# The first blocks of a fused macaron layer: normalization on another engine, ternary weights in quarters, and matmuls ahead of the first work

## The chip, the cores and the metric

The kernel runs on one core of one Trainium2 chip. A core has five engines, each with its own queue of instructions that it works off in order: PE (TensorE, matrix multiplication; its weight loads are shown as PEld), DVE (VectorE), ACT (ScalarE), POOL (GpSimd) and SP (SyncE, which here issues transfers only). They wait for each other through semaphores. SBUF is the working memory, 128 partitions wide, and PSUM the memory into which PE writes.

The metric is the device time of one execution in microseconds (us). The median of three runs of the kernel before is 625.42 us (625.16 to 626.89).

## The reference

An input x of 16 sequences of 256 tokens with 256 features goes through three residual blocks: half a feed-forward network (FFN), causal attention with 16 heads and rotary positions, and the same half FFN again. In front of each block stands a layer normalization. The weights of the FFN are made ternary first: each entry becomes -1, 0 or 1, by a threshold of half the mean absolute value of the whole matrix.

```python
def _bit_quant(w):
    scale = jnp.maximum(jnp.mean(jnp.abs(w)), EPS)
    w_ternary = jnp.clip(jnp.round(w / scale), -1.0, 1.0)
    return w + jax.lax.stop_gradient(w_ternary - w)
...
h = jnp.einsum('bsd,fd->bsf', x, w1q) + b1
h = jax.nn.gelu(h, approximate=False)
return jnp.einsum('bsf,df->bsd', h, w2q) + b2
...
x = x + 0.5 * _L0_ffn_ref(_layernorm(x, axis=-1), w1, b1, w2, b2)
x = x + _L0_attn_ref(_layernorm(x, axis=-1), Wq, Wk, Wv, Wo)
x = x + 0.5 * _L0_ffn_ref(_layernorm(x, axis=-1), w1, b1, w2, b2)
```

A layer normalization subtracts from each token its mean over the 256 features and multiplies by rstd, one over the root of its variance plus 1e-5.

## The kernel before

The 4096 tokens stand in SBUF for the whole kernel, as eight blocks `xs[0]` to `xs[7]` of 512 tokens (four tiles of 128 tokens each). All engines are called through `InOrder`, so that each engine's instructions stand in the order in which the program text issues them: what a line waits for, everything behind it on the same engine waits for too.

**Loads.** SP issues the loads in the order: first half of block 0, half of w1, the bias b1, w2, the bias b2, blocks 1 to 7, and then the attention's weights. ACT's queue issues the other half of block 0 and of w1. Meanwhile POOL sets the constants: the identity for transposes, `averaging` (a 128x128 matrix of one value), masks, `power` (the exponent -0.5).

**The FFN.** `ffn(ln, after)` makes one pass: `ln` is 0 for the first FFN and 2 for the second. `begin` does what precedes the first step, and `step(u)` is called for u = 0 to 65. Step u = 8 i + f does `up(i, f)` for block i and slice f of the 1024 hidden features (128 of them), and `down(i, f)` of the step two before (LATE = 2). `up` is four matmuls of 128x512 into a PSUM tile `m` (two of them at a time), then ACT's Gelu twice (`h_high`, in the rounded format that PE takes fast, and `h_whole`), and then the difference `h_rest`, on POOL for slices 1, 3 and 5 and on DVE otherwise. `down` is eight matmuls of 128x256 (`w<-w2q,h_high` and `w<-w2q,h_rest`). After the last slice of a block DVE adds the result to x.

**What has to be there first.** For each block: `stats` (two DVE instructions a tile), `finish_stats` (two POOL instructions of 128x4, `var` and `rstd`), `prepare` (four normalized tiles `xn`, by `normalize` on DVE), and `turn_in` twice (four transposes on PE, a cast on ACT, a difference on DVE), which gives `xnT`, what `up` multiplies. For block 1 all statistics are taken at step 1, `prepare` stands at step 3, and the `turn_in`s at steps 5 and 6, between `up` and `down`. For block 2 the statistics stand at steps 4 to 7, and so on.

For the weights: `sizes(n)` sums the absolute values of w1 (n = 0) or w2 (n = 1) by partition, `threshold(n)` sums over the partitions by two small matmuls with `averaging` and makes `half[n]`, and `signs(n, part)` makes the ternary values of a part by two DVE instructions. Before, these are halves of the matrix:

```python
signs(0, lambda w: w[:, :, 0 : FF // 2])        # in begin
signs(0, lambda w: w[:, :, FF // 2 :])          # in begin
if ln == 0 and u in (0, 3):                     # in step
    part = slice(0, NFC // 2) if u == 0 else slice(NFC // 2, NFC)
    signs(1, lambda w: w[:, part, :])
```

`add_bias(i)` lets POOL add half of b2 to the block's x, before the FFN's result is added.

**Behind the first FFN** the attention is written out in slots, which begin while the first FFN's last steps run, and then the second FFN. None of that is touched.

Of the kernel before, what the change touches and what calls it, by code (L numbers as in the profile page):

```python
# [8 lines left out]
FP = mybir.dt.float32  # L9
FR = mybir.dt.float32r  # L10
AF = mybir.ActivationFunctionType
ALU = mybir.AluOpType
# [17 lines left out]
def kernel(  # L30
# [144 lines left out]
    def tokens(n):  # L175
        return xs[n // BT][:, n % BT, :]

    def stats(ln, n):
        st = small.tile([P, 6], FP, name="st")
        vector.bn_stats(st, tokens(n))  # L180
        vector.bn_aggr(mv[ln][:, n, :], st)

    def finish_stats(ln, first, n):

        var = small.tile([P, BT], FP, name="var")
        gpsimd.tensor_scalar(
            var[:, 0:n], mv[ln][:, first : first + n, 1], LN_EPS, 1.0, ALU.add, ALU.mult
        )
        gpsimd.tensor_tensor(
            rstd[ln][:, first : first + n], var[:, 0:n], power[:, 0:n], ALU.pow  # L190
        )

    def normalize(ln, n, to, engine=None):
        (engine or vector).tensor_scalar(
            to,
            tokens(n),
            mv[ln][:, n, 0:1],
            rstd[ln][:, n : n + 1],
            ALU.subtract,
            ALU.mult,  # L200
        )
# [6 lines left out]
    def sizes(n):  # L208
        for k in range(2):
            part = (flat1, flat2)[n][:, k * FF : (k + 1) * FF]  # L210
            total = totals[n][:, k : k + 1]
            if n == 0 and k == 0:
                vector.tensor_reduce(total, part, AX.X, ALU.add, apply_absolute_value=True)
            else:

                size = w2q[:, k * NFC // 2 : (k + 1) * NFC // 2, :]
                scalar.activation(
                    size.rearrange("p k d -> p (k d)"), part, AF.Abs, accum_out=total
                )

    def threshold(n):
        mean = ps_mm.tile([P, 1], FP, name="mm")
        for k in range(2):
            total = totals[n][:, k : k + 1]
            tensor.matmul(mean, averaging, total, start=(k == 0), stop=(k == 1))

        for k, factor in enumerate((0.5, -0.5)):
            vector.tensor_scalar(
                half[n][:, k : k + 1], mean, QUANT_EPS, factor, ALU.max, ALU.mult
            )  # L230

    def signs(n, of):

        w, to = of((w1, w2)[n]), of((w1q, w2q)[n])
        vector.tensor_scalar(to, w, half[n][:, 1:2], None, ALU.is_lt)
        vector.scalar_tensor_tensor(
            to, w, half[n][:, 0:1], to.bitcast(FP), ALU.is_gt, ALU.subtract
        )
# [34 lines left out]
    def ffn(ln, after):  # L273
        xn, xnT, hT, ys = {}, {}, {}, {}

        def measure(i):
            if ln == 0:
                for t in range(BT):
                    stats(0, i * BT + t)
                finish_stats(0, i * BT, BT)  # L280

        def prepare(i, engine=None):
            xn[i] = fp.tile([P, BT, D], FP, name="xn", bufs=1)
            for t in range(BT):
                normalize(ln, i * BT + t, xn[i][:, t, :], engine)
            xnT[i] = [fp.tile([P, KC, TB], FR, name=f"xnT_{n}") for n in range(2)]

        def add_bias(i):
            gpsimd.tensor_add(xs[i], xs[i], b2_sb.unsqueeze(1).to_broadcast([P, BT, D]))

        def turn_in(i, k):
            tp = ps_mm.tile([P, TB], FP, name="mm")
            for t in range(BT):
                tensor.transpose(
                    tp[:, t * P : (t + 1) * P], xn[i][:, t, k * P : (k + 1) * P], ident
                )
            high, rest = (xnT[i][n][:, k, :] for n in range(2))
            scalar.copy(high, tp)
            return lambda: vector.tensor_sub(rest, tp, high.bitcast(FP))

        def up(i, f):
            h = ps_m.tile([P, TB], FP, name="m")
            for n in range(2):
                for k in range(KC):
                    tensor.matmul(
                        h,
                        w1q[:, k, f * P : (f + 1) * P],
                        xnT[i][n][:, k, :],
                        start=(n == 0 and k == 0),
                        stop=(n == 1 and k == KC - 1),  # L310
                    )
            high = fp.tile([P, TB], FR, name="h_high", bufs=LATE + 3)
            rest = fp.tile([P, TB], FR, name="h_rest", bufs=LATE + 3)
            whole = fp.tile([P, TB], FP, name="h_whole", bufs=3)
            scalar.activation(high, h, AF.Gelu, bias=b1_sb[:, f : f + 1])
            scalar.activation(whole, h, AF.Gelu, bias=b1_sb[:, f : f + 1])

            engine = gpsimd if f in (1, 3, 5) and not (ln == 0 and i == NBLK - 1) else vector
            engine.tensor_sub(rest, whole, high.bitcast(FP))
            hT[i, f] = (high, rest)  # L320

        def down(i, f):
            if f == 0 and ln == 2 and i == NBLK - 1:

                ys[i] = [ps_mm.tile([P, 2, D], FP, name="mm") for t in range(0, BT, 2)]
            elif f == 0:
                y = ps_w.tile([P, BT, D], FP, name="w")
                ys[i] = [y[:, t : t + 2, :] for t in range(0, BT, 2)]
            parts = hT.pop((i, f))
            order = [(t, n) for t in range(BT) for n in range(2)]  # L330
            if ln == 2 and (i, f) == (NBLK - 1, NFC - 1):

                order = [(t, n) for n in range(2) for t in range(BT)]
            for t, n in order:

                tensor.matmul(
                    ys[i][t // 2][:, t % 2, :],
                    parts[n][:, t * P : (t + 1) * P],
                    w2q[:, f, :],
                    start=(f == 0 and n == 0 and t % 2 == 0),  # L340
                    stop=(f == NFC - 1 and n == 1 and t % 2 == 1),
                )
            if f == NFC - 1:
                for t in range(0, BT, 2):
                    xt = xs[i][:, t : t + 2, :]
                    vector.scalar_tensor_tensor(
                        xt, ys[i][t // 2], 0.5, xt, ALU.mult, ALU.add
                    )
                for t in range(0, BT, 2):
                    after(i, t)  # L350

        def begin():
            measure(0)
            if ln == 0:
                sizes(0)
            prepare(0)
            if ln == 0:
                threshold(0)
                signs(0, lambda w: w[:, :, 0 : FF // 2])
            for k in range(KC):  # L360
                turn_in(0, k)()
            if ln == 0:
                signs(0, lambda w: w[:, :, FF // 2 :])
                sizes(1)

        def step(u):
            i, f = divmod(u, NFC)
            if i < NBLK:
                up(i, f)
                if ln == 0 and u == 0:  # L370
                    threshold(1)
                if ln == 0 and u in (0, 3):
                    part = slice(0, NFC // 2) if u == 0 else slice(NFC // 2, NFC)
                    signs(1, lambda w: w[:, part, :])
                if ln == 0 and u == 4:
                    gpsimd.tensor_scalar(b2_sb, b2_sb, 0.5, 0.0, ALU.mult, ALU.add)
                if u == 1:
                    measure(1)
                if ln == 0 and f >= 4 and i + 2 < NBLK:
                    stats(0, (i + 2) * BT + f - 4)  # L380
                    if f == NFC - 1:
                        finish_stats(0, (i + 2) * BT, BT)
                if i + 1 < NBLK:
                    if f == 3:
                        prepare(i + 1)
                    if f in (5, 6):
                        turn_in(i + 1, f - 5)()
                if f == (1 if i == NBLK - 1 else 6):
                    add_bias(i)
            if u >= LATE:  # L390
                down(*divmod(u - LATE, NFC))
            if ln == 0 and u == 2 * NFC + 2:
                make_tables()
            if ln == 0 and u < (NBLK - 1) * NFC and later:
                later.pop(0)()

        return begin, step, prepare, turn_in
# [423 lines left out]
```

## Time and profile before

| What | us |
|---|---|
| median of three runs (lowest, highest) | 625.42 (625.16, 626.89) |
| the profiled execution | 622.22 |
| its span, from the first to the last instruction | 620.4 |
| PE busy | 599.5 |
| DVE busy | 461.2 |
| ACT busy | 416.3 |
| POOL busy | 300.9 |

A profile is one execution, recorded instruction by instruction. Its span is shorter than the time of that execution, as the time also holds what lies around the first and the last instruction. All start times below count from the span's start. Every compute instruction of the kernel is recorded under line 167, the helper `traced`, so instructions are told apart by their tiles: `xn<-x,mv,rstd` is the instruction that writes `xn` from x, mean and variance, and rstd. A row of the timeline gives start, time from the first start to the last end, engine, line, operation, tiles, shapes and the number of instructions merged in it; in brackets, the time that the engine was idle before, and what ended it. "issue" is time in which an engine waited for nothing that the profile shows.

### The profile page before, as it was taken

Reading aid. Unit: us, or ns where it says so; the run is one execution under the profiler, and the core shown is the slowest. Engines: PE = TensorE matmul, PEld = TensorE weight load, DVE = VectorE, ACT = ScalarE, POOL = GpSimd, SP = SyncE. Lnnn points to the kernel's source line nnn. Section 1 sums busy time; section 2 is a strip of 40 time slices with the busy share of each in tenths; the row PEclk is TensorE's granted clock in tenths of the full one; section 3 lists DMA queues with packets and bytes.
Section 4 is the critical chain, followed back from the end, with each engine's and each line's share of the span. In section 5 each row is a group of like instructions: output and inputs, shape, how many; then the busy total and the mean of one; then the engine's idle time right before and its main releaser. Section 6 shows DMA issues by size and latency. Waiting matters only on the chain.

```text
span 620.4 us, 14716 instructions
## 1 busy us (share of the span) xinstructions
PE 599.5 (97%) x5580; PEld 486.6 (78%) x5580; DVE 461.2 (74%) x1654; ACT 416.3 (67%) x716; POOL 300.9 (49%) x273
## 2 busy tenths in 40 slices
PE   4999999999999999999999999999998999999997
PEld 3798999887667777777777777777766798888886
DVE  6877777786788888888888888888886465555553
ACT  4666766664576677676777677767765676676674
POOL 3655555782464455545564456453430243334443
PEclk9999999999999999999999999999999999999999
DMA  8800000000001000100001000100100011011001
GB/s 285 180 22 1 2 1 18 17 1 18 20 35 38 19 21 36 38 27 29 19 36 38 20 20 36 37 20 21 36 4 2 1 35 35 34 35 35 27 21 55
DMA packets 25478, 21.30 MB, mean 34 GB/s; under 512 B 10944, under 2 KB 21056, under 8 KB 25408
## 3 DMA queue, kind: packets, MB, share of 16 engines
q1 hardware_dynamic: 24848, 19.44, 9.8%
q8 instruction: 44, 0.72, 0.5%
q10 hardware_dynamic: 560, 0.92, 0.4%
q14 instruction: 26, 0.21, 0.1%
HBM read 7.51 MB, written 4.19 MB: 19 GB/s over the span
## 4 chain that ended last, share of the span: by engine, by line
PE 89%; DVE 5%; ACT 3%; issue 1%; DMA 1%; POOL 1%; DVEq 0%; SPq 0%; POOLq 0%
PE mm L167 38%; PE w L167 29%; PE m L167 22%; DMA w<-in_w1T_dram 1%; DVE h_rest L167 1%; DVE xn L167 1%; ACT h_high L167 1%; ACT h_whole L167 1%; DVE w2q L167 1%; DVE st L167 1%; DVE w L167 0%; DVE x L167 0%; DVE masked L167 0%; DVE mv L167 0%; ACT pT L167 0%
## 5 line engine op out<-in xcount | busy, mean ns | idle before, releaser
L167 DVE CUSTOM_DVE_ANT_0 masked<-m,mask_q 128x128 f32<-128x128 f32 x480 | 142.7, 354 | 41.0 <-PE m L167 39.7
L167 PE MATMUL m<-xnT,w1q 128*128 128x512 f32 x512 | 145.1, 404 | 0.8 <-ACT xnT L167 0.7
L167 ACT ACTIVATE h_high<-m,b_sb 128x512 fp32r<-128x512 f32 x128 | 88.5, 691 | 78.2 <-PE m L167 78.1
L167 DVE TENSOR_TENSOR h_rest<-h_whole,h_high 128x512 fp32r<-128x512 f32 x83 | 75.0, 904 | 72.0 <-ACT h_whole L167 71.5
L167 ACT ACTIVATE pT<-w 128x768 f32<-128x768 f32 x128 | 104.1, 815 | 31.4 <-DVE w L167 24.9
L167 PE MATMUL w<-qT,kT 32*128 32x256 f32 (+1 forms) x1024 | 120.6, 348 | 1.9 <-ACT pT L167 1.8
L167 PE MATMUL w<-w2q,h_high 128*128 128x256 f32 x480 | 120.8, 285 | 0.7 <-DVE w2q L167 0.7
L167 PE MATMUL w<-w2q,h_rest 128*128 128x256 f32 x480 | 117.8, 279 | 0.4 <-POOL h_rest L167 0.3
L167 PEld LDWEIGHTS w<-qT,kT 32*128 32x128 f32 x1024 | 89.9, 184 | 33.0 <-issue 25.9
L167 PE MATMUL m<-kT,qT 32*128 32x128 f32 x960 | 114.9, 349 | 0.7 <-ACT kT L167 0.7
L167 POOL TENSOR_TENSOR h_rest<-h_whole,h_high 128x512 fp32r<-128x512 f32 x45 | 60.1, 1335 | 108.5 <-ACT h_whole L167 108.4
L167 PEld LDWEIGHTS m<-xnT,w1q 128*128 128x128 f32 x512 | 88.3, 190 | 16.7 <-DVE xnT L167 2.9
L167 PEld LDWEIGHTS w<-w2q,h_rest 128*128 128x128 f32 x480 | 90.4, 188 | 5.1 <-POOL h_rest L167 0.7
L167 PEld LDWEIGHTS w<-w2q,h_high 128*128 128x128 f32 x480 | 90.3, 188 | 5.2 <-DVE w2q L167 1.2
L167 DVE TENSOR_TENSOR w<-w,mask_k 128x512 f32<-128x512 f32 x128 | 88.8, 695 | 7.1 <-PE w L167 7.0
L167 ACT ACTIVATE h_whole<-m,b_sb 128x512 f32<-128x512 f32 x128 | 87.3, 682 | 0.0
L167 PEld LDWEIGHTS m<-kT,qT 32*128 32x128 f32 x960 | 65.9, 185 | 2.9 <-ACT kT L167 1.6
L167 POOL TENSOR_TENSOR w<-w,cosT 128x512 f32<-128x512 f32 x32 | 41.3, 1292 | 51.8 <-ACT w L167 31.9
L167 PE MATMUL mm<-xnT_a,wqk 128*128 128x256 f32 x256 | 62.2, 386 | 0.0
L167 POOL TENSOR_SCALAR var<-mv 128x4 f32<-128x4 f32 (+1 forms) x32 | 6.9, 216 | 106.2 <-DVE mv L167 105.6
L167 POOL TENSOR_TENSOR w<-w,sinT 128x512 f32<-128x512 f32 x32 | 41.0, 1280 | 26.0 <-DMA w<-w 25.9
L167 PEld LDWEIGHTS mm<-xnT_a,wqk 128*128 128x128 f32 x256 | 46.1, 190 | 7.6 <-issue 0.7
(86 smaller groups left out, 918.9 us busy)
## 6 DMA issues: line engine op xcount, KB each, us to landing
w<-w SPq DMA_DIRECT2D x64, 128.0 KB
out_dram<-x SPq DMA_DIRECT2D x15, 256.0 KB
x<-in_x_dram SPq DMA_DIRECT2D x7, 512.0 KB
w<-in_w2T_dram SPq DMA_DIRECT2D x1, 1024.0 KB
qT<-mT SPq DMA_DIRECT2D x64, 4.0 KB
w<-in_w1T_dram SPq DMA_DIRECT2D x1, 512.0 KB
w<-in_w1T_dram ACTq DMA_DIRECT2D x1, 512.0 KB
wqk<-in_wqkvT_dram SPq DMA_DIRECT2D x16, 32.0 KB
```

Of the source, the lines that this page charges most:

```text
L167: return tc.keep_in_program_order(getattr(self.engine, name)(*args, **kwargs))
```

## The change

Five things are changed, all in the first FFN's `begin` and in its steps 0 to 9.

1. `turn_on(n)`: n matmuls of `averaging` with itself, into a tile of the PSUM pool `m`, whose result nobody reads. 20 of them stand ahead of everything on PE, four more between the transposes of block 0 and step 0.
2. `prepare` takes blocks 0 and 1 to ACT: POOL makes the offsets `less` = -mean x rstd (two more instructions of 128x4 behind `rstd`), and ACT writes xn = rstd x x + less, one instruction a tile. On block 1 this moves from step 3 to step 4.
3. `signs` works on quarters. The first quarters of w1 and of w2 stand where the first halves stood (that of w2 now ahead of the `h_rest` of step 0), and the others follow at the end of `begin` and at steps 1 to 5 by the table `soon`.
4. The statistics of block 1 are taken one tile a step at steps 1 to 4, between quarters, and finished at step 4. Those of block 2 move from steps 4 to 7 to steps 8 and 9, two tiles a step.
5. `add_bias(0)` moves from step 6 to step 7.

```diff
+    def turn_on(n):
+        on = ps_m.tile([P, P], FP, name="m")
+        for _ in range(n):
+            tensor.matmul(on, averaging, averaging, start=True, stop=True)
...
         def prepare(i, engine=None):
             xn[i] = fp.tile([P, BT, D], FP, name="xn", bufs=1)
+            at = slice(i * BT, (i + 1) * BT)
+            if engine is scalar:
+                less = small.tile([P, BT], FP, name="less")
+                gpsimd.tensor_scalar(less, mv[ln][:, at, 0], -1.0, 0.0, ALU.mult, ALU.add)
+                gpsimd.tensor_mul(less, less, rstd[ln][:, at])
             for t in range(BT):
-                normalize(ln, i * BT + t, xn[i][:, t, :], engine)
+                n = i * BT + t
+                if engine is scalar:
+                    scalar.activation(
+                        xn[i][:, t, :],
+                        tokens(n),
+                        AF.Identity,
+                        bias=less[:, t : t + 1],
+                        scale=rstd[ln][:, n : n + 1],
+                    )
+                else:
+                    normalize(ln, n, xn[i][:, t, :], engine)
...
             scalar.activation(whole, h, AF.Gelu, bias=b1_sb[:, f : f + 1])
+            if ln == 0 and (i, f) == (0, 0):
+                threshold(1)
+                signs(1, quarter(1, 0))
...
+        def quarter(n, k):
+            at = slice(2 * k * P, 2 * (k + 1) * P) if n == 0 else slice(2 * k, 2 * (k + 1))
+            return (lambda w: w[:, :, at]) if n == 0 else (lambda w: w[:, at, :])
+
+        soon = {
+            1: ((1, 1), 0),
+            2: ((0, 2), 1),
+            3: ((0, 3), 2),
+            4: ((1, 2), 3),
+            5: ((1, 3), None),
+        }
 
         def begin():
             measure(0)
-            if ln == 0:
-                sizes(0)
-            prepare(0)
-            if ln == 0:
-                threshold(0)
-                signs(0, lambda w: w[:, :, 0 : FF // 2])
+            turn_on(20)
+            sizes(0)
+            prepare(0, scalar)
+            threshold(0)
+            signs(0, quarter(0, 0))
             for k in range(KC):
                 turn_in(0, k)()
-            if ln == 0:
-                signs(0, lambda w: w[:, :, FF // 2 :])
-                sizes(1)
+            turn_on(4)
+            signs(0, quarter(0, 1))
+            sizes(1)
 
         def step(u):
             i, f = divmod(u, NFC)
             if i < NBLK:
                 up(i, f)
-                if ln == 0 and u == 0:
-                    threshold(1)
-                if ln == 0 and u in (0, 3):
-                    part = slice(0, NFC // 2) if u == 0 else slice(NFC // 2, NFC)
-                    signs(1, lambda w: w[:, part, :])
+                if ln == 0 and u in soon:
+                    part, t = soon[u]
+                    if u == BT:
+                        stats(0, BT + t)
+                        finish_stats(0, BT, BT)
+                        prepare(1, scalar)
+                    signs(part[0], quarter(*part))
+                    if u < BT:
+                        stats(0, BT + t)
...
-                if u == 1:
-                    measure(1)
-                if ln == 0 and f >= 4 and i + 2 < NBLK:
+                if ln == 0 and u in (NFC, NFC + 1):
+
+                    for t in range(0, BT, 2):
+                        stats(0, 2 * BT + t + u - NFC)
+                    if u == NFC + 1:
+                        finish_stats(0, 2 * BT, BT)
+                if ln == 0 and f >= 4 and 0 < i and i + 2 < NBLK:
...
-                    if f == 3:
+                    if f == 3 and (ln, i) != (0, 0):
                         prepare(i + 1)
...
-                if f == (1 if i == NBLK - 1 else 6):
+                if f == (1 if i == NBLK - 1 else 7 if ln == 0 and i == 0 else 6):
                     add_bias(i)
```

## The prediction

> **What bounds the kernel now.** I read the page first, to see whether an engine or a wait sets the time.
>
> ```profile
> span 620.4 us, 14716 instructions
> ...
> PE 599.5 (97%) x5580; PEld 486.6 (78%) x5580; DVE 461.2 (74%) x1654; ACT 416.3 (67%) x716; POOL 300.9 (49%) x273
> ...
> PE   4999999999999999999999999999998999999997
> DVE  6877777786788888888888888888886465555553
> ...
> PE 89%; DVE 5%; ACT 3%; issue 1%; DMA 1%; POOL 1%; DVEq 0%; SPq 0%; POOLq 0%
> ```
>
> PE is busy in tenths 9 from the second of 40 slices to nearly the last, and 89% of the chain that ended last is PE's. Only the first slice (15.5 us) is half empty. PE's queue has a fixed order, so once it is dense, whatever the start gains or loses moves every later matmul by the same amount. The change touches the first 11 of the 66 steps of the first FFN pass, so I forecast one number: when PE begins the second token block, step 8. Before, that is at 30.54 us (the timeline's `m<-xnT,w1q` of that step). Next the chain of waits between 16 and 27 us, to see what paces PE there.
>
> ```profile
> 16.78 1.28 DVE w2q L167
> ...
> 19.68 0.32 DVE st L167
> ...
> 20.03 0.18 DVE mv L167
> 20.21 0.57 DVE h_rest L167
> 20.79 0.68 DVE w2q L167
> ...
> 21.49 1.28 DVE w2q L167
> 22.77 1.81 DVE xn L167 x2
> 24.58 0.04 issue
> 24.62 0.97 PE mm L167 x3
> 25.59 0.94 PE w L167 x8
> 26.53 0.92 PE m L167 x4
> ```
>
> Until 24.6 us the chain is DVE's: ternary values of w2, statistics of block 1, `h_rest`, the other half of w2, then `xn`, the normalized block 1. From the transposes of `xn` (PE mm) on it is PE's. So DVE paces the start, and the transposes of block 1 are where it hands over. Third, the timeline around that point, by engine.
>
> ```profile
> 20.30 0.54 POOL L167 TENSOR_SCALAR var<-mv 128x4 f32<-128x4 f32 x1 [1.09 <-DVE mv L167]
> 20.92 1.40 POOL L167 TENSOR_TENSOR rstd<-var,power 128x4 f32<-128x4 f32 x1
> 22.29 1.64 POOL L167 TENSOR_TENSOR h_rest<-h_whole,h_high 128x512 fp32r<-128x512 f32 x1
> ...
> 22.69 2.52 DVE L167 TENSOR_SCALAR xn<-x,mv,rstd 128x256 f32<-128x256 f32 x4
> ...
> 24.23 1.37 PE L167 MATMUL mm<-ident,xn 128*128 128x128 f32 x4 [0.23 <-DVE xn L167]
> ```
>
> The statistics of block 1 end at 20.21; POOL makes rstd of them by 22.32, hidden behind the second half of w2 on DVE; DVE starts `xn` at once when it is free, and PE loses only some tenths at the transposes. Last, rows for prices: ACT on a 128x256 tile with a bias and a scale column, and PE early against PE later.
>
> ```profile
> 163.42 0.59 ACT L167 ACTIVATE kT<-w,one,own 128x256 f32<-128x256 f32 x1
> 163.91 0.50 ACT L167 ACTIVATE qT<-w,own 128x256 f32<-128x256 f32 x1
> ...
> 14.30 3.08 PE L167 MATMUL m<-xnT,w1q 128*128 128x512 f32 x8
> ...
> 22.90 1.09 PE L167 MATMUL m<-xnT,w1q 128*128 128x512 f32 x4
> ```
>
> Eight early matmuls take 3.08 us, eight later ones 2 x 1.09 = 2.18: PE starts slow and is at speed by 18 us.
>
> **The change, part by part.** *Normalization of block 0 moves from DVE to ACT.* POOL's rstd ends at 6.63 + 1.03 = 7.66. Two new POOL operations follow: the negated mean, like `var` (0.20, and 0.08 between), and a product of 128x4, which no row shows: between `var`'s 0.20 and the power's 1.03, and nearest to the first; I take 0.30. Offsets at 8.32. Four ACT operations like `kT` (0.59, starts 0.49 apart): 8.37 + 3 x 0.49 + 0.59 = 10.43, against 9.36 on DVE. Before, the transposes began only at 9.06 and ran at 1.95 / 8 = 0.24 each; at later speed (27.30 us: four in 0.60) the last four end near 11.0, so the second cast starts at 11.1 against 11.04. ACT's two sums over w2 follow it, and the second is there at 13.8 against 13.72. Worth nothing: +0.1.
>
> *Warm-up matmuls.* 20 run from 1.07 us, when `averaging` is set. The threshold's two matmuls left four records in 0.98, so a 128x128 one may be two records of 0.12 (late speed) to 0.25 (early): 5 to 10 us, to end between 6 and 11. The next needed matmul is at 8.22; a late end would push step 0 past 13.8, where step 1 waits for the sums anyway, so 0 to +0.8; I take 0. What they may buy is 3.08 - 2.18 = 0.9 us in steps 1 and 2.
>
> *DVE's queue, re-cut.* A half of w1 or w2 costs 0.79 + 1.20 between starts (15.99, 16.78, 17.98). For a quarter: first operation 0.48, interpolated between 0.33 (`xn` at 7.99, 256 wide) and 0.79; second 0.66, above half of 1.20 and by the 128x512 subtractions (0.57 to 0.66). 1.15 a pair; bounds 1.00 and 1.35. A tile's statistics cost 0.53 (18.54 to 19.07). Then: sums at 13.8, threshold 14.4, two half-thresholds 0.25: 14.65. First quarter of w2: 15.8. `h_rest` of step 0 (0.6): 16.4. Second quarter 17.55; statistics 18.1; `h_rest` of step 2 waits for ACT, 18.25 to 18.85 (step 2's matmuls end at 16.5 at full speed; ACT does two steps of 1.28 behind 15.75). Third quarter of w1: 20.0; step 4 needs it, and PE is there at 19.45. Step 4 starts at 20.05, against 21.04 before: a gain of 1.0 up to here. Statistics 20.55, last quarter of w1 21.7, statistics 22.2, then `h_rest` of step 4, whose ACT work ends 2.4 after the matmuls began (21.04 to 22.17, + 1.28): 22.45 to 23.1. Only now the fourth statistics: 23.65, against 20.21 before. They were moved past a quarter of w1, two waits for ACT and a step of PE.
>
> *Block 1's normalization behind them.* `var` and rstd took 1.31 on a quiet chip (6.35 to 7.66) and 2.02 beside DVE (20.30 to 22.32); the two new ones 0.66, or 1.0 by the same ratio. 2.0 to 3.0; DVE then runs w2's last quarters, so 2.5: 26.2. The new wait stands in ACT's queue: `xn` of block 1 is ahead of step 5's two Gelus, and ACT has nothing else from 22.45 on. Four operations, 2.06: 28.3. Queued behind on PE is everything: step 5's matmuls end near 23, then come the transposes that wait for `xn`, and `down` of step 3 behind them. That one starts at 28.45; before it started at 25.35. That is +3.1. From there to step 8 took 5.19 before, and the chain there is PE's; the later Gelus (29.5), cast (30.0) and `h_rest` (30.8) are each in time for it.
>
> *Contention.* `xn` on DVE took 1.37 alone and 2.52 beside a POOL subtraction, 1.15 more. The last quarter of w1 stands beside POOL's `h_rest` of step 3 (19.9 to 21.4): 0 to 0.85; I take 0.4.
>
> *Parts at nothing.* The statistics of block 2 come two a step at steps 8 and 9 and rstd behind them; DVE has up to 0.9 idle a step there (34.54 and 36.70 us), the transposes wait until step 13, and if that cover fails it costs up to 0.5. The first bias a step later stands in the same place of POOL's queue, directly behind step 5's subtraction, as no POOL work was between: 0. SP's queue is the same. Constants: no line of the diff moves one.
>
> Sum: 0.1 is inside the 3.1, + 0.4 = +3.5. The profiled execution has 622.22 us, of which 620.4 span; its changed twin would be 625.7. The median of the runs is 625.42, 3.2 above the profiled one, with no row to say why; I add the same 3.5 to it: 628.9. Bounds: pairs 1.00 (three before step 4: -0.45), POOL 2.0 (-0.5), no contention (-0.4): +2.1. Pairs 1.35 (+0.6), POOL 3.0 (+0.5), contention 0.85 (+0.45), step 0 late (+0.5): +5.5.
>
> **PE's speed after the pause.** PE would stand from 23 to 26.7, and transpose sparsely to 28.4. Of rows: after 8.2 us of idleness PE was slow, after its longest later wait (1.1 us, for `pT`) it was not; this pause lies between. The price, if slow again, is again eight matmuls' 0.9, up to twice that.
>
> The Trainium skill ("TensorE: Matmul & The Clock Gate", Part 1: The HAM clock gate) says that one idle window of about 3.4 us halves the clock until a busy one has passed. By that rule the pause may trip it and an estimate would be 1 to 2 us on top; by the rows alone it stays open. The rule also speaks for the 20 early matmuls.
>
> **Rivals.** *The pause and slow matmuls behind it*: +3.5 + 0.9 to 1.8, or 629.8 to 630.7. For it: a pause three times the longest seen; against: transposes break it. *The start decides, not slower*: DVE loses 1.37 + 2.52 us of `xn`, PE is at speed from step 0, step 4 comes 1.0 earlier, and the fourth statistics reach POOL by 20.2, so that block 1 is ready at step 5: 625.42 - 1.0 = 624.4. It decides if the fourth statistics end before 20.6; against it, step 4's Gelu stands ahead of them. If the unprofiled runs' 3.2 us are slow early matmuls, it could reach 622.5. *No difference*: stall and speed cancel (a pause shorter by 2), 625 to 627.
>
> **Numbers.** The stall at full speed 0.55; with slow matmuls 0.22; the start decides 0.12; no difference 0.11. Most likely 628.9, its own range 627.5 to 630.9. Over all cases 8 in 10 lie from 626.0 to 631.2. A change below 0.3% (1.9 us) can't be told from none. Faster gets 0.09 (most of the start's 0.12), same 0.14 (no difference, and the rest of the start's), slower the two stalls, 0.77.
>
> **What would show it.** Right: ACT idle some 4 us before the `xn` of 20 to 30 us, released by POOL; a PE wait of over 3 us at `mm<-ident,xn`; step 8 at 33.5 to 34.5; step 4 near 20. Wrong: rstd of block 1 before 23, or no PE gap there; the first `m` matmuls still at 0.39 each.

## The result, and the profile after

| | before | after |
|---|---|---|
| median of six runs (lowest, highest), us | 626.12 (624.84, 627.0) | 632.32 (631.13, 635.12) |
| the profiled execution, us | 622.22 | 632.96 |
| its span, us | 620.4 | 631.2 |
| step 8 (the second token block) begins, us | 30.54 | 38.31 |

After over before is 1.0113, interval 1.0089 to 1.0137: slower by 1.1%, 6.2 us. Forecast were +3.5 and 628.9, in a range from 626.0 to 631.2: the direction is right, the size too small.

Single runs of the kernel before fall into groups that go with their mean granted PE clock (.998 to 1.00: 622.2 to 622.6; .996: 623.7 to 624.0; .993 and .994: 624.6 to 625.5; .990: 626.6 to 627.7), for a reason that the experiment with late matmuls shows below, so that its median lies anywhere between 624.8 and 626.6, by which runs are taken.

The page of after, first, in the lines shown of before:

```profile
span 631.2 us, 14827 instructions
...
PE 611.5 (97%) x5628; PEld 496.6 (79%) x5628; DVE 460.1 (73%) x1654; ACT 419.3 (66%) x724; POOL 300.9 (48%) x277
...
PEclk8889999999999999999999999999998999999999
...
PE 87%; DVE 5%; ACT 2%; issue 1%; POOL 1%; DVEq 0%; POOLq 0%
```

PE is busy 12 us longer than before, with 48 more records of matmuls; those took 8.1 us (6.25 + 1.89 in the timeline) and lie mostly in its idle start. Its share of the chain that ended last fell from 89% to 87%. The PEclk row says what else there is: the clock is below full in the first three of the 40 slices and once late. A busy PE at half clock is lost time that a busy share does not show. Then the chain of waits (start, length, what):

```profile
17.74 1.67 DVE w2q L167
...
20.98 1.64 DVE w1q L167
...
22.76 1.19 PE m L167 x4
...
24.56 0.69 ACT h_whole L167
...
25.27 0.69 DVE h_rest L167
25.96 0.35 DVE st L167
...
27.02 1.52 POOL rstd L167
...
29.23 0.61 ACT xn L167
...
31.83 1.71 PE w L167 x8
33.54 1.68 PE m L167 x4
```

This is the forecast's chain, item by item: ternary quarters, step 4 on PE, its Gelu on ACT, its `h_rest` on DVE, only then the fourth statistics (`st`), POOL's rstd and offsets, ACT's `xn`. Two things in it were not forecast: the two DVE operations of 1.6 us, and four `m` matmuls of 1.68 us behind the pause, where before's took 0.92. The timeline at the handover, and the granted clock by stretch (columns: stretch and its length; busy time and instructions of PE, PEld, DVE, ACT, POOL; granted clock, DMA share, GB/s):

```profile
29.23 2.07 ACT L167 ACTIVATE xn<-x,less,rstd 128x256 f32<-128x256 f32 x4 [3.99 <-POOL less L167]
29.88 1.95 PE L167 MATMUL mm<-ident,xn 128*128 128x128 f32 x4 [4.07 <-ACT xn L167]
33.34 1.89 PE L167 MATMUL m<-xnT,w1q 128*128 128x512 f32 x4
36.44 1.09 PE L167 MATMUL m<-xnT,w1q 128*128 128x512 f32 x4
```

```profile
4.35:11.18 6.83, 5.32 (x40) 4.47 (x40) 4.64 (x13) 3.48 (x7) 2.46 (x7) 1.00 0.94 308
11.18:14.59 3.41, 3.41 (x15) 3.02 (x14) 2.43 (x4) 2.90 (x6) 0.00 (x0) 0.50 1.08 368
14.59:28.24 13.65, 8.79 (x49) 6.83 (x47) 12.30 (x25) 6.22 (x10) 4.23 (x4) 1.00 0.90 217
28.24:35.07 6.83, 5.14 (x17) 3.77 (x18) 1.31 (x2) 3.69 (x7) 3.71 (x6) 0.50 0.44 65
...
485.60:489.00 3.40, 3.40 (x40) 1.84 (x36) 0.70 (x1) 1.41 (x4) 0.00 (x0) 0.50 0.00 0
```

ACT idles 3.99 us for POOL's `less` and PE 4.07 us for ACT's `xn`: the pause is there, as long as forecast. While PE stands, the clock is halved, at 28.24, and stays so for 6.83 us, just where the queue behind the pause has to be worked off. All edges lie on a grid of 3.41 us (28.24 to 35.07 is two of them, 11.18 to 14.59 one). The Trainium skill ("TensorE: Matmul & The Clock Gate", Part 1: The HAM clock gate) says that the gate looks at free-running windows of about that length, and that PE stays at half rate until it has been busy for one: the grid agrees.

So +7.77 us at step 8. At step 60 it is 150.0 against 141.7, +8.3, and the half clock at 485.6, 3.4 us at half speed, accounts for about 1.7 more of the 10.7 between the two executions. The rest, some 1.2 with the 0.5 between steps 8 and 60, is spread thinly over the dense part: from step 19 to step 29 the starts of `m<-xnT,w1q` lie 19.77 us apart in after and 19.64 in before. All eleven kernels recorded here with POOL's offsets and ACT's `xn` show 19.77 or 19.78, all six without them 19.63 to 19.65. No row shows how that part of the change reaches matmuls so far behind it; the cause stays open.

### The profile page after: what moved, and what is told of

Same layout as the page of the kernel before. It is cut to its first block, busy times and chain, and to the rows that moved or that the text cites. A ratio compares the mean times of both kernels' runs of the same rounds, so it can differ in the third digit from the quotient of the medians.

```text
span 631.2 us, 14827 instructions
## 1 busy us (share of the span) xinstructions
PE 611.5 (97%) x5628; PEld 496.6 (79%) x5628; DVE 460.1 (73%) x1654; ACT 419.3 (66%) x724; POOL 300.9 (48%) x277
## 4 chain that ended last, share of the span: by engine, by line
PE 87%; DVE 5%; ACT 2%; issue 1%; POOL 1%; DVEq 0%; POOLq 0%
PE mm L167 37%; PE w L167 29%; PE m L167 22%; DVE h_rest L167 1%; ACT h_whole L167 1%; ACT h_high L167 1%; DVE xn L167 1%; DVE w2q L167 1%; DVE st L167 0%; POOL rstd L167 0%; DVE w L167 0%; DVE x L167 0%; DVE masked L167 0%; DVE w1q L167 0%; ACT pT L167 0%
## 5 line engine op out<-in xcount | busy, mean ns | idle before, releaser
L167 PE MATMUL w<-w2q,h_high 128*128 128x256 f32 x480 | 122.5, 287 | 0.0
L167 PE MATMUL w<-w2q,h_rest 128*128 128x256 f32 x480 | 120.2, 283 | 0.2 <-POOL h_rest L167 0.2
```

The lines of the kernel that those rows point to most:

```text
L167: return tc.keep_in_program_order(getattr(self.engine, name)(*args, **kwargs))
```

## The experiments

The theory after the result: the fourth statistics come too late (the pause), the pause halves the clock (some 1.5 us), and on the way there DVE loses time beside POOL (some 1.8 us). Rivals: the early matmuls push step 0 back and do harm; w1's last quarters, now at steps 2 and 3, hold PE; the normalization on ACT costs by itself, wherever it stands. A number that tells more than the whole time is the start of step 8 in the profile, as PE is dense behind it; it does not tell all, as ACT's normalization alone shows below.

**The pause filled: the clock's share.** After, with 16 matmuls of `averaging` ahead of block 1's transposes.

```diff
+if ln == 0 and u == 5:
+    fill = ps_mm.tile([P, P], FP, name="mm")
+    for _ in range(16):
+        tensor.matmul(fill, averaging, averaging, start=True, stop=True)
```

> The changed kernel with 16 more matmuls of averaging with itself between step 5's matmuls and the transposes of block 1, to fill PE's pause of 4.07 us. If the granted clock of 0.52 from 28 to 35 us costs time beside the pause itself: the clock stays at 1.00 there, step 8 begins near 36.7 instead of 38.3 (from the first block 1 transposes' end to step 8 took 6.7, before 5.2), and the time falls by 1.5 to 630.8. If the pause alone counts and the slow matmuls hide in the waits behind it: step 8 stays at 38, time within 0.5 of 632.3.

Step 8 began at 36.78, 1.5 earlier than in after. In the windows of this kernel:

```profile
28.00:35.00 7.00, 6.00 (x43) 5.03 (x42) 1.64 (x3) 4.98 (x10) 3.88 (x6) 1.00 0.46 69
482.70:493.00 10.30, 9.72 (x59) 6.27 (x56) 2.02 (x4) 4.20 (x6) 0.50 (x1) 0.50 0.01 2
```

The clock is 1.00 from 28 to 35, so the half clock cost 1.5 us there; the fourth statistics still ended at 26.64. The median did not fall (634.4 against 626.57, ratio 1.012, 1.0069 to 1.017): the second line shows three windows of half clock at 482.7 in this execution, 450 us away from the edit. One of its four runs, at a mean clock of .997 (the others .989), took 629.62.

**The statistics of block 1 at step 1 again.** The quarters stay, block 1 is normalized on ACT at step 4 as in after.

```diff
 if u == BT:
-    stats(0, BT + t)
-    finish_stats(0, BT, BT)
     prepare(1, scalar)
 signs(part[0], quarter(*part))
-if u < BT:
-    stats(0, BT + t)
+if u == 1:
+    measure(1)
```

> The changed kernel with the four statistics of block 1 at step 1, as before, and all else changed. If the spread-out statistics set the pause: the fourth ends near 21.5 instead of 26.5, block 1's xn on ACT follows step 4's Gelu directly, the transposes start near 26.5 instead of 29.9, the clock holds, step 8 begins at 33 to 34, time 627 to 628.5. If it is the quarters beside POOL's h_rest that are late, or ACT's xn: transposes not before 28.5, step 8 at 37 or later, time 631 or more.

Its timeline:

```profile
21.51 0.18 DVE L167 BATCH_NORM_AGGREGATE mv<-st 128x2 f32<-128x6 f32 x1
23.60 1.16 PE L167 MATMUL m<-xnT,w1q 128*128 128x512 f32 x4 [3.12 <-DVE w1q L167]
25.96 1.57 ACT L167 ACTIVATE xn<-x,less,rstd 128x256 f32<-128x256 f32 x3
```

629.34 (626.11 to 631.43), ratio 1.0063 (1.0032 to 1.0093); the time expected was 627 to 628.5. The fourth statistics ended at 21.69 instead of 26.5, `xn` began at 25.96 instead of 29.23, and step 8 at 33.6: 4.7 of the 7.8 us are back. No other single edit of after gave back as much: the place of the statistics is the largest single part. But PE then waited 3.12 us for `w1q` at step 4 (23.6), and the half clock followed there, from 24.78 to 28.19.

**Without the early matmuls.**

```diff
-turn_on(20)
...
-turn_on(4)
```

> The changed kernel without its 24 early matmuls. If they buy speed for steps 0 to 2: 0.9 slower, 633.2. If the four ahead of step 0 (1.89 us at a clock of 0.53) hold step 0 back by about as much as the others buy: within 0.7 of 632.3, and step 0 begins near 11.8 instead of 12.7. The pause at block 1's transposes is the same in both.

631.75 (631.49 to 635.14), ratio 1.0107 (1.0064 to 1.0151). Step 0 came 0.9 earlier (11.81 for 12.70), step 4 0.45 earlier, and step 8 at 38.56: what comes earlier ends in the same pause (4.25 us). They do neither harm nor good here, but not because nothing else moves. Without them PE is slow for longer: at 17 us its 128x512 matmuls still begin 0.42 apart, in after 0.23. And DVE meets POOL elsewhere: the two operations that took 1.67 and 1.63 in after take 0.75 each here, and one of 0.45 takes 1.13 instead. With 1.1 us less of such stretching, the fourth statistics still ended at 26.23, only 0.3 earlier.

**The early matmuls alone, in the kernel before.**

```diff
 measure(0)
+turn_on(20)
...
     turn_in(0, k)()
+turn_on(4)
```

> The kernel before with the 24 early matmuls alone. If they buy the early slow matmuls: 0.5 to 0.9 faster than before, 625.2 to 625.6, step 8 near 29.8 instead of 30.5. If DVE paces the start anyway (the chain of before is DVE's from 15.7 to 24.6): no difference, 626.1, step 8 at 30.5. Slower by up to 1 if the four ahead of step 0 run slow.

625.79 (622.7 to 629.54), ratio 0.9999 (0.9967 to 1.0031). Its best runs, at full clock, took 622.7, before's best 622.2. Its profile is that of its slowest run (629.54), with step 8 at 32.61, 2.1 later than before's. There PE runs ahead, then waits 2.65 us for `w2q`, and the clock is halved behind it, and once more late:

```profile
17.90:24.70 6.80, 6.08 (x22) 5.57 (x23) 6.63 (x15) 1.27 (x2) 2.86 (x3) 0.50 0.92 228
478.70:488.90 10.20, 9.58 (x58) 6.27 (x56) 1.94 (x3) 4.17 (x6) 0.42 (x1) 0.50 0.01 2
```

In the first stretch DVE is busy 6.63 of 6.80 us. It sets the pace there, so a PE that is earlier only waits longer, and here loses its clock by it.

**w1's four quarters ahead of step 0.** After, with all of w1 in `begin` as before.

```diff
-2: ((0, 2), 1),
-3: ((0, 3), 2),
+2: (None, 1),
+3: (None, 2),
...
-signs(0, quarter(0, 1))
+for k in (1, 2, 3):
+    signs(0, quarter(0, k))
```

> The changed kernel with all four quarters of w1 ahead of step 0; block 1's statistics still one a step. If the w1 quarters between the statistics make the fourth one late: step 4 no longer waits 2.4 us for w1 and begins near 21.0, but the w2 threshold and its first quarter come 2.4 us later on DVE, so the fourth statistics gain 1 us at most (25.5 instead of 26.5), the transposes start near 28.8, step 8 near 37, time 1 below the changed kernel. If w1's late quarters were the whole matter: fourth statistics by 22.5, step 8 by 33.5, time 627.

635.12 (632.93 to 636.92), ratio 1.0161 (1.0114 to 1.0208): a miss, no gain. Step 4 began at 22.49 (22.76 in after), the fourth statistics at 26.17, step 8 at 38.31 as in after. The work has only changed places in DVE's queue. Two of the four runs have a mean clock of .982 and took 636.6 and 636.9; the profiled one, 632.93, has .988.

**w1's quarters and the statistics both put back**, the edits of this experiment and of the one with the statistics.

```diff
+for k in (1, 2, 3):
+    signs(0, quarter(0, k))
...
+if u == 1:
+    measure(1)
```

> As the run before it, and block 1's statistics all at step 1. If two causes add, w1's late quarters and statistics tied to the steps: the transposes start near 24.8, the clock holds from 14 us on, step 8 begins at 31.2 to 32, time within 1.5 of before (626 to 628). If ACT's xn or POOL's offsets still cost by themselves: a PE wait of over 1.5 us remains at the transposes, step 8 at 33 or later.

630.3 (628.59 to 631.79), ratio 1.008 (1.0049 to 1.011); step 8 at 33.71, no better than with the statistics alone. PE now waited 2.33 us for `w2q` (16.49), with the half clock behind it (19.77 to 23.18), and the offsets stood in POOL's queue behind its `h_rest` of step 3, so that `xn` began at 26.27. In front of the transposes PE waited only 0.21.

**POOL's differences given to DVE: the contention.** After, with the `h_rest` of steps 1 and 3 on DVE.

```diff
-engine = gpsimd if f in (1, 3, 5) and not (ln == 0 and i == NBLK - 1) else vector
+engine = gpsimd if f in (1, 3, 5) and not (ln == 0 and (i == NBLK - 1 or (i, f) in ((0, 1), (0, 3)))) else vector
```

> The changed kernel with the h_rest of steps 1 and 3 on DVE instead of POOL. If POOL's subtraction beside them stretches DVE's second ternary operation (1.67 and 1.63 us where others of the shape take 0.75): all of that shape take 0.75, DVE pays two subtractions of 0.6 more, and step 4 begins 0.3 to 0.6 earlier than 22.76. If the stretch has another cause: 1.6 stays.

In after, the timeline of DVE's second ternary operation beside POOL's difference, and without it:

```profile
15.96 0.75 DVE L167 SCALAR_TENSOR_TENSOR w2q<-w,half,w2q 128x512 fp32r<-128x512 f32 x1
17.50 1.37 POOL L167 TENSOR_TENSOR h_rest<-h_whole,h_high 128x512 fp32r<-128x512 f32 x1 [9.11 <-ACT h_whole L167]
17.74 1.67 DVE L167 SCALAR_TENSOR_TENSOR w2q<-w,half,w2q 128x512 fp32r<-128x512 f32 x1
20.76 1.31 POOL L167 TENSOR_TENSOR h_rest<-h_whole,h_high 128x512 fp32r<-128x512 f32 x1 [1.89 <-ACT h_whole L167]
20.98 1.63 DVE L167 SCALAR_TENSOR_TENSOR w1q<-w,half,w1q 128x512 fp32r<-128x512 f32 x1
23.58 0.75 DVE L167 SCALAR_TENSOR_TENSOR w1q<-w,half,w1q 128x512 fp32r<-128x512 f32 x1
```

The same two operations in this experiment:

```profile
18.86 0.75 DVE L167 SCALAR_TENSOR_TENSOR w2q<-w,half,w2q 128x512 fp32r<-128x512 f32 x1
21.18 0.75 DVE L167 SCALAR_TENSOR_TENSOR w1q<-w,half,w1q 128x512 fp32r<-128x512 f32 x1
```

1.67 and 1.63 become 0.75. That is the contention, 0.92 + 0.88 = 1.80 us, shown on DVE's queue. But DVE now does the two differences itself, so step 4 gained only 0.69 (22.07), and step 8 (38.26) nothing: the half clock still began behind the pause, at 28.78. One run only, 631.0.

**Late matmuls in the kernel before: where its own times part.** Before's profiled execution kept its clock to the end, but most of its runs have a lower mean clock, and the variant with early matmuls alone, which is the same kernel there, shows where: three windows of half clock at 478.7 to 488.9. Just ahead, in the timeline of before, PE has two small waits at the end of the attention's last block:

```profile
473.76 1.62 PE L167 MATMUL w<-qT,kT 32*128 32x256 f32 x16 [1.10 <-ACT pT L167]
...
476.64 0.92 PE L167 MATMUL w<-qT,kT 32*128 32x256 f32 x8 [0.68 <-ACT pT L167]
```

The experiment puts four matmuls into the first and three into the second, and changes nothing else.

```diff
 for p in range(8):
+    if p in (3, 5):
+        turn_on(4 if p == 3 else 3)
     weigh = scores(z, p, None, None)
```

> The kernel before with 4 and 3 matmuls of averaging with itself in PE's two waits near 473 and 476 us, behind the attention's last block. Most executions of the kernel before show a granted clock of 0.990 to 0.994 and 624.6 to 627.2 us, some 0.998 and 622.2; in other kernels' traces the loss is a stretch of half clock that begins at 478 to 486 us. If the thin PE work there is what loses the clock: nearly all executions show 0.998 or more, and the median falls by 3 to 4, to 622.5. If not: median 626, plus the matmuls where they don't fit the waits, 0 to 0.5.

622.45 (622.2 to 623.72, ten runs, clock .997 to 1.00) against 625.9 for before measured beside it, ratio 0.9964 (0.994 to 0.9988). Its timeline:

```profile
472.64 1.06 PE L167 MATMUL m<-averaging 128*128 128x128 f32 x8
473.91 1.62 PE L167 MATMUL w<-qT,kT 32*128 32x256 f32 x16 [0.21 <-ACT pT L167]
...
475.96 0.83 PE L167 MATMUL m<-averaging 128*128 128x128 f32 x6
```

The work behind starts when it did, and yet the kernel is 3.4 us faster, because the clock is no longer halved behind it. The profiles say the same: of the nine without late matmuls five show half clock between 478 and 493 us (after, the filled pause, the early matmuls alone, and both runs with w1's quarters ahead of step 0), of the eight with them none does. So before loses 0 to 5 us there, more in one execution and less in another (622.2 to 627.7), and this is a version faster than both kernels. It also gives a quiet base: all experiments that follow stand on it.

**The whole change on this base**: after, with the same three lines.

```diff
 for p in range(8):
+    if p in (3, 5):
+        turn_on(4 if p == 3 else 3)
```

> The whole change on the same base (late matmuls at 473 and 476 us). If the whole difference comes from the start: step 8 near 38, 7.5 to 8 later than the base, and half a microsecond behind it; median 630.5 to 631.5, so +8 to +9 against 622.45, where the medians without the late matmuls show +6.2. If the parts merely add, the three runs above give +6 to +6.5, and the rest is the half clock behind the pause, 1.5.

631.85 (631.49 to 632.45), 9.4 above the base, where 8 to 9 were expected; step 8 at 38.54, against 30.63 in the base. Compared without the late chance, the change costs 9.4 us and not 6.2. Between the two profiles 7.9 of it are there at step 8, and another 1.3 gather evenly behind it, where half a microsecond was expected: in the dense part a step begins every 1.88 or 1.89 us here and every 1.87 in the base, the spread that after shows too.

**ACT's normalization alone**, for blocks 0 and 1 at their old places, with POOL's offsets.

```diff
-prepare(0)
+prepare(0, scalar)
...
-prepare(i + 1)
+prepare(i + 1, scalar if (ln, i) == (0, 0) else None)
```

> The kernel before with the late matmuls at 473 and 476 us (622.45), and one part of the change: blocks 0 and 1 normalized on ACT with POOL's offsets, at their old places (block 1 at step 3). If ACT's normalization costs by itself: the offsets wait behind POOL's subtraction of step 3, xn of block 1 begins near 24.3 instead of 22.7, step 8 near 31.6 instead of 30.6, time 623.5. If the relief of DVE (1.37 and 2.5 us) pays: step 8 at 30 or before, 622.

627.67 (627.39 to 628.97), +5.2 where about one was expected: a miss. The timeline of the first surprise and the chain of the second:

```profile
17.35 2.37 DVE L167 SCALAR_TENSOR_TENSOR w2q<-w,half,w2q 128x1024 fp32r<-128x1024 f32 x1
17.37 1.26 POOL L167 TENSOR_TENSOR h_rest<-h_whole,h_high 128x512 fp32r<-128x512 f32 x1 [9.06 <-ACT h_whole L167]
19.77 0.39 PE L167 MATMUL w<-w2q,h_high 128*128 128x256 f32 x1 [2.85 <-DVE w2q L167]
```

```profile
22.57 1.40 POOL rstd L167
23.96 1.60 POOL h_rest L167
...
25.65 0.19 POOL less L167
...
25.93 0.21 POOL less L167
26.14 0.03 issue
26.16 2.08 ACT xn L167 x4
```

DVE's operation took 2.37 (1.28 in the base) because it now met POOL's difference; PE waited 2.85 and lost its clock from 21.07 to 24.48. And the two offsets, 0.2 each, stood behind POOL's `h_rest` of step 3: rstd was there at 23.97, `xn` began at 26.16, and step 8 at 33.76. In this profile, that of a run of 628.48, step 8 is 3.1 later than in the base and the end 6.1. Behind step 8 another meeting follows: DVE's `h_rest` at 32.28 took 2.54 (0.69 alone) beside POOL's addition of the bias (31.86, 2.41), and PE waited 1.38 for `xnT`, which makes it +4.8 at step 9; the last 1.3 are the slightly longer steps again. So ACT's normalization with POOL's offsets does cost by itself, by where it puts POOL's work.

**Quarters alone**, in the order of `soon`, with the first quarter of w2 ahead of the `h_rest` of step 0.

```diff
-signs(0, lambda w: w[:, :, 0 : FF // 2])
+signs(0, quarter(0, 0))
...
+soon = {1: (1, 1), 2: (0, 2), 3: (0, 3), 4: (1, 2), 5: (1, 3)}
...
+if ln == 0 and u in soon:
+    signs(soon[u][0], quarter(*soon[u]))
```

> The same base and one part: the ternary values by quarters at the change's places; statistics at step 1, normalization on DVE. If the quarters of w1 moved behind step 1 hold PE: a wait of 2 to 3 us for w1q ahead of step 4, which begins near 23.5 instead of 21.1, step 8 near 33, time 625. If quarters are harmless without the other parts: step 4 within 0.5 of 21.1, time 622.5 to 623.

625.46 (625.1 to 626.86), +3.0, as expected. Step 4 waited 3.14 us for `w1q` (22.41), with the half clock from 23.11 to 26.52; step 8 at 32.38, 1.8 late. The rest is one more meeting with POOL's addition of the bias: DVE's `h_rest` took 1.79 at 31.27, and PE waited 1.00 for `xnT` behind step 8.

**Statistics one a step alone**, and block 1 normalized at step 4, on DVE.

```diff
-if u == 1:
-    measure(1)
+if ln == 0 and 1 <= u <= BT:
+    stats(0, BT + u - 1)
+    if u == BT:
+        finish_stats(0, BT, BT)
+        prepare(1)
```

> The same base and one part: block 1's statistics one a step at steps 1 to 4, normalized at step 4 on DVE; block 2's at steps 8 and 9. If tying the fourth statistics to step 4's Gelu is the pause: they end near 24 instead of 20.3, rstd near 26, the transposes start near 26.3 instead of 24.3, step 8 at 32.6 to 33.5, time 624.5 to 625.5. If DVE only does the same work in another order: step 8 within 0.5 of 30.6.

629.44 (628.8 to 631.11), +7.0 where 2 to 3 were expected: the mechanism was hit, the size missed. Its timeline, and its clock from 26.5 on:

```profile
24.57 0.18 DVE L167 BATCH_NORM_AGGREGATE mv<-st 128x2 f32<-128x6 f32 x1
...
26.09 1.27 POOL L167 TENSOR_TENSOR h_rest<-h_whole,h_high 128x512 fp32r<-128x512 f32 x1
26.16 4.34 DVE L167 TENSOR_SCALAR xn<-x,mv,rstd 128x256 f32<-128x256 f32 x4 [1.41 <-POOL rstd L167]
27.65 0.45 PE L167 MATMUL mm<-ident,xn 128*128 128x128 f32 x1 [3.61 <-DVE xn L167]
29.90 1.12 PE L167 MATMUL mm<-ident,xn 128*128 128x128 f32 x3 [1.81 <-DVE xn L167]
```

```profile
26.50:33.30 6.80, 3.84 (x14) 3.19 (x15) 4.68 (x5) 0.59 (x1) 3.20 (x2) 0.50 0.56 80
```

The fourth statistics end 4.5 us later than before's 20.21, `xn` on DVE takes 4.34 beside POOL's work, and two windows of half clock follow the pause. The parts alone cost 5.2, 3.0 and 7.0, in sum 15.2; together 9.4. Each part alone has a wait and a stretch of half clock of its own, the whole change one pause with one stretch behind it; that is why, as far as the traces tell, their prices do not add.

**Two causes taken out of the whole change** (on the base, 631.85): the statistics at step 1, and the `h_rest` of steps 1 and 3 on DVE.

```diff
+if u == 1:
+    measure(1)
...
-engine = gpsimd if f in (1, 3, 5) and not (ln == 0 and i == NBLK - 1) else vector
+engine = gpsimd if f in (1, 3, 5) and not (ln == 0 and (i == NBLK - 1 or (i, f) in ((0, 1), (0, 3)))) else vector
```

> The whole change with the late matmuls (631.85), block 1's statistics back at step 1, and the h_rest of steps 1 and 3 on DVE. If the pause and the stretch are most of it: all second ternary operations take 0.75, the fourth statistics end near 21, rstd on POOL by 23.6, xn on ACT follows step 4's Gelu at 25.3, no half clock after 15 us, step 8 near 32.8 instead of 38.5, time 624.7 to 625.7. If ACT's normalization is a cause of its own: step 8 at 35 or later, 627 or more.

626.73 (626.31 to 627.26): 5.1 of the 9.4 us are gone, one less than the least expected. The second ternary operations took 0.75, but for one of 0.93 at 23.92; the fourth statistics ended at 21.13; step 8 at 34.22, and ACT's `xn` followed step 4's Gelu at 26.28 without a pause of PE at the transposes. What remained begins at step 4: PE waited 3.05 us for `w1q` there, and the clock was halved for two windows:

```profile
22.10:29.00 6.90, 5.97 (x21) 5.13 (x21) 5.19 (x9) 3.69 (x7) 2.06 (x4) 0.51 0.57 68
```

**And w1's quarters ahead of step 0 as a third.**

```diff
-signs(0, quarter(0, 1))
+for k in (1, 2, 3):
+    signs(0, quarter(0, k))
```

> As the run before it, and w1's four quarters ahead of step 0. If w1's late quarters are the third cause: no wait for w1q at step 4, xn of block 1 near 24.1, step 8 near 31.6, time 623.5 to 624.5. If DVE merely has the same work in another order: as the run before it, 625.

626.74 (625.71 to 628.02): a miss, no gain. The wait of 3.05 for `w1q` turned into one of 1.45 for `w2q` at 16.63, with the half clock from 19.32 to 22.73; step 8 came 1.5 earlier, at 32.74 in this profile (itself a run of 625.84), but five of its ten runs lie at 627.4 to 628.0.

**A version from what was learnt**: the base, with w2's threshold and first half ahead of the `h_rest` of step 0, and the `h_rest` of step 3 on DVE.

```diff
+if ln == 0 and (i, f) == (0, 0):
+    threshold(1)
+    signs(1, lambda w: w[:, 0 : NFC // 2, :])
```

> The kernel before with the late matmuls, w2's threshold and first half ahead of step 0's h_rest, and the h_rest of step 3 on DVE instead of POOL. If DVE's idle 0.9 us around that h_rest (14.8 to 15.7) and POOL's subtraction beside xn (2.52 instead of 1.37 us) cost what the trace shows: the transposes of block 1 start 0.8 earlier, step 8 at 29.6 to 30.0 instead of 30.6, time 621.5 to 622. If DVE only trades one wait for another: 622.45.

622.52 (622.17 to 623.78), ratio to before 0.9957 (0.9937 to 0.9977), but the same as the base's 622.45: no gain. Step 4 began 0.37 earlier than in the base (20.74) and step 8 0.14 later (30.77, where 29.6 to 30.0 were expected): DVE traded one wait for another.

## Why the prediction was right and wrong

**The mechanism was right.** Block 1's normalization waits for the fourth statistics, these stand behind step 4's Gelu and `h_rest`, and the wait ends in a PE pause at the transposes. Undoing this one place gave back 4.7 us at step 8. POOL's four small operations took 2.7 us from the statistics to the offsets (forecast 2.5), ACT's four `xn` 2.07 (2.06). The pause took 4.07, where 3.7 were forecast (23 to 26.7); that this is so close is luck in part, as both of its ends came some three us late (25.8 to 29.9). The early matmuls ended at 7.37 and held up no threshold. Statistics of block 2 and the bias cost nothing that the trace shows.

**The step that failed: the likeliest case let PE go on at full speed behind the pause, and the sum leading to it was mis-sized.** `down` of step 3 was forecast for 28.45 + 0.4 = 28.85 and came at 31.48; from there to step 8 were 5.19, and it took 6.83. The 4.3 us between forecast (34.0) and trace (38.31), added up along the chain's rows, are:

- *Contention*: taken as 0.4, measured 1.80, so 1.4. The forecast looked at one meeting of DVE and POOL, by `xn`'s 1.15. There are two, with w2's second quarter (0.92) and w1's third (0.88).
- *w2's threshold*: first quarter at 15.43, not 14.65, 0.8. ACT's sums over w2 ended at 14.08, not 13.8, and the threshold's matmuls stood behind step 0, which began at 12.70 for 11.75: the four matmuls ahead of it, left out of the sum, took 1.89 us at half clock. They are not the whole of it: without any early matmuls step 0 began at 11.81, but the sums ended at 14.69 and the first quarter began at 15.69. "Worth nothing: +0.1" for block 0 on ACT rested on transposes at later speed, which that run did not have.
- *Half clock behind the pause*: left out of the likeliest case, 1.6 by the trace, and 1.5 by filling the pause. The rival that had it (0.22) priced it well, at 0.9 to 1.8, but stood on the same short sum, so its 629.8 to 630.7 fell short too.
- Some 0.5 in small amounts on the path from w2's second quarter to `xn`.

This is an account of where the rows differ from the forecast, not of what each would give back: both meetings taken away (contention) or the early matmuls taken away gave step 8 nothing, filling the pause 1.5, the statistics at step 1 4.7.

The forecast also let whatever the start loses move every later matmul by the same amount. It does not: behind step 8 the change lost 1.3 us more, by slightly longer steps.

What the early matmuls were to buy, 0.9 us in steps 1 and 2, they nearly bought: the eight matmuls took 2.35 us for before's 3.08. Step 0, 0.95 later, cancelled it.

Step 4, forecast 1.0 earlier than before, came 1.7 later (22.76), by the first two items of the list: the quarters were no gain even up to there, and PE waited 2.44 us for `w1q`.

**The base was wrong as well.** The forecast put +3.5 on the median and had "no row to say why" the profiled execution was 3.2 faster. The late matmuls gave the reason: in most runs before loses its clock for some windows behind 478 us. So +7.8 at step 8 shows as +6.2 in the medians, as +10.7 between the two profiled executions, and as +9.4 in the medians with late matmuls in both.

**The rivals.** "The start decides" is out: its condition, statistics by 20.6, was missed by 6, and the one experiment with early matmuls alone shows why speed at the start buys nothing, as PE runs into DVE's queue. "No difference" is out.

**Open.** Of the 9.4 us, 5.1 are the place of the statistics and the two meetings with POOL, with the half clock that followed them. Of the other 4.3, some 1.2 are the longer steps behind step 8, found in every kernel with ACT's normalization and POOL's offsets and not explained. How the remaining 3 divide between offsets in POOL's queue, the order of the quarters, and the half clock behind each wait for DVE was not separated: each edit moved the wait and its window to another place.

## What to carry to other kernels

Where a queue is paced by one engine, moving a late-needed small piece (four statistics) behind work that waits for others costs the whole round trip; follow the piece's own deadline before cutting large ones finer. Price a PE wait with the half clock that can follow it, 3.41 us or two times that at half speed: in these profiles every wait of 2.65 us or more that was left unfilled (eleven, behind the first work) had it, and of eight between 1.29 and 2.44, at full clock until then, two had it. Price a meeting of a DVE operation with a POOL operation at what POOL still has to run, less 0.2 us. Sort single runs by granted clock before reading differences of some us: seven useless matmuls in two waits were worth 3.4 us, while neither edit of before's start (early matmuls; w2's threshold earlier) was worth any.

## What the runs showed of the hardware

- **DVE stands still beside POOL.** POOL's difference ended at 18.87 and 22.07 in after; DVE's operations beside it ended 0.54 later in both cases, though they had begun at 17.74 and 20.98 and take 0.75 alone. In the run with ACT's normalization alone it is 19.72 against 18.63, with 1.28 alone, though there DVE's row begins 0.02 ahead of POOL's. The ends fit a DVE that is blocked until POOL is done, less some 0.2 us that overlaps. The Trainium skill ("SBUF — State Buffer", Who interferes with whom) states such a lock between a GpSimd operation that reads SBUF and a DVE operation with two SBUF inputs; these ends agree. `xn`, which reads one tile, is held too: four took 4.34 beside POOL's two operations in the run with the statistics one a step, 1.37 alone. The statistics, beside POOL's difference at 17.74 in before, kept their 0.39 to 0.42.
- **A thin PE loses its clock too.** At 470 to 479 us before's longest wait is 1.10 us, and still the clock fell in most runs. The Trainium skill ("TensorE: Matmul & The Clock Gate", Part 1: The HAM clock gate) speaks of an idle window; here, where the runs decide, windows with short waits and small matmuls were enough, and with seven matmuls of 128x128 ten runs of ten had a mean clock of .997 or more.
- **Where a trace has no clock record, the view's 1.00 cannot be read as full speed.** The first record in before's trace begins at 16.47 us, and the windows ahead of it read 1.00; yet step 0's four matmuls took 2.05 us, as in after at a recorded 0.50 (2.03), and 1.09 later.
